# The first half sequence of a state-space recurrence moved into the attention stage before it, with its states summed by adding DMAs, and one expert layer issued at two tiles a unit

## The chip, the cores and the metric

One core of one Trainium2 chip runs the whole program. The engines are PE (matrix multiply; PEld is its weight load), DVE, ACT, POOL (elementwise and activation engines; only PE, DVE and ACT reach PSUM) and SP, which issues most transfers. The metric is device time in microseconds, median of repeated executions: 2376.53 us before (17 runs, 2367.86 to 2383.13).

## The reference, cut to what matters

Four layers over a batch of B = 4 sequences of T = 1024 positions with D = 128 features, in float32; each layer is a mixer and a feed-forward part, each followed by a residual sum and a layer norm. The change touches the third layer and the start of the fourth.

```python
# layer 2 mixer: causal linear attention, 16 heads of 64, q and k weighted by cos and sin of the position
S_cos = S_cos + kc[..., :, None] * v[..., None, :]          # state, step by step over T
num = einsum(qc, S_cos) + einsum(qs, S_sin); den = sum(qc*z_cos + qs*z_sin)
out = num / max(den, 1e-6)
# layer 2 feed-forward: 8 experts, top 2 by softmax; a gated pair and a product per expert
h13 = x @ w13[e]; gate, up = split(h13); y = (silu(gate) * up) @ w2[e]
# layer 3 mixer: a selective state-space recurrence, E = 256 channels, N = 16 states
xs = silu(conv(x @ in_w.T)); delta = softplus(xs @ wd1.T @ wd2.T + b); Bm = xs @ wb.T; Cm = xs @ wc.T
h = exp(delta[:, :, None] * A) * h + (delta * x)[:, :, None] * b[:, None, :]
y = einsum('ben,bn->be', h, c)                              # sum over the 16 states
y = ((y + xs * W_D) * silu(skip)) @ out_w.T
# layer 3 feed-forward: 8 experts, all computed, weighted by a top-p gate
```

## The kernel before

The activations stay in SBUF: `xN[b]` with positions on the partitions, `xT[b]` with features on them.

**Attention (`l2_attn`).** The work is 128 units: for each batch element four quarters of 256 positions, for each quarter eight pairs of heads. The loop runs t from -2 to 131 and issues in each round the parts of neighbouring units: `l2_keys` (t+1: transposes of k into bank `kp`, then kN on ACT), `l2_project` (t+2: q and k in a `pj` bank, r_q and r_k on ACT, the two qt products on POOL, needed two units later), `l2_scores` (t+1: banks pa0 and pa1, then the products `a` on DVE), `l2_before` and `l2_within` (t: all matmuls into the two `po` banks), `l2_sums` (t+1: state sums, bank `kp`, then st on DVE), and `l2_out` (t: dn, its reciprocal and the product co on DVE, which read po). Generators in the list `side` get one step a round: values of the next quarter, `l2_project_out` (transposes and bank `pr`), the norm, and after a batch element's last quarter `l2_dispatch`. PE's order in this loop is the written one (`manual_schedule` for PE); the orders of ACT, DVE, POOL and SP are chosen by a planner from its own simulated times, within the data dependencies.

**PSUM.** There are eight banks of 512 float32 columns. Two are `pj`, two are one tile `po` (of whose banks 130 columns each are used), and four are each shared by two uses: pa0 with m0, pa1 with m1, kp with mo, pr with sx. Accesses of different engines to one bank are put in order, also when they touch different columns.

**Expert layer of layer 2 (`l2_dispatch`, `l2_ffn`).** For each batch element the router ranks the experts (`router`, lines 1220 to 1254), positions are counted, and 16 indirect transfers on POOL scatter the rows to DRAM (L1383). `l2_ffn` is a generator (`moe`) over 4 x 23 = 92 tiles of 128 rows; one step issues the loads for tile t+8, the weights of t+4 (384 KB on SP, L1458, four buffers), the row transposes of t+2, the gated pair of t (`l2_hidden`: m0, m1; tanh on ACT L1490, products on DVE) and the second matmul of t-2 (`l2_expert_out`: mo, ys). After an element's last tile `l2_combine` gathers the rows back with 16 indirect transfers on POOL (L1529) and norms them; then its `st["done"]` is set. In the attention one step a unit is issued, once element 0's rows have been put, until element 1 is done.

**Recurrence (`l3_prepare`, `l3_scan`, `l3_sum`, `l3_finish`).** The 4 x 2 half sequences ("halves") of 512 positions are worked through one after the other, channels on the partitions, two column blocks ec. `l3_prepare` makes xs, delta (`dl`), delta times xs (`ud`), and writes B and C as 32 `rows` to DRAM. `l3_scan` does for each of the 16 states n: two loads on SP that broadcast a row to all partitions (bn, cn, 256 KB each, L1840), db = ud x bn on POOL (L1845), for each ec an exponential on ACT into PSUM (da, L1849) and a scan on DVE (L1850), a copy of the last column to `carry`, hc = db x cn on POOL (L1861). The sum over the states is made on PE by identity matmuls into two banks (pys); for b > 0 two states are first added by an accumulating transfer from POOL's queue (L1865). `l3_finish` applies the gate, the output projection, norm and router, and hands the half to the experts of layer 3 (`l3_experts`, `l3_ffn`: weights wh, matmuls ph and py, ReLU hh), of which each scan step issues three pieces while `moe` has work and four afterwards. Before, half 0 is prepared inside the attention (`l3_early`, at one step a unit once element 0 is done, with its large tiles laid over `xT[0]` to `xT[2]`), and its scan begins after the attention; during it `moe` gets two steps a state, later one.

## Time and profile before

| | us |
|---|---|
| median of 17 runs | 2376.53 (2367.86 to 2383.13) |
| the profiled execution, its own time | 2376.19 |
| its span, first to last instruction | 2374.3 |
| first and last dn of the attention (128) | 646.9 and 1374.1 |
| first db multiply of half 0, half 1, half 2 (POOL) | 1426.3, 1530.9, 1622.5 |
| last hc multiply of half 7 ends | 2233.1 |
| mean granted TensorE clock | 0.909 of full |

In a window's row the columns are: start and end in us from the span's start, its length, then for PE, PEld, DVE, ACT and POOL the busy us and the number of instructions, then the granted TensorE clock, the share of the DMA engines that was busy, and GB/s. In a row of the timeline: start, us, engine, line, operation, tile written <- tiles read, count, and in brackets idle time ahead of it with what ended it. In a row of waits: engine, tile and line that waited, what it waited for, total us, times, longest us. A unit's time is read from one dn to the next (dn is issued once a unit); single units: 36 took 11.2 us (815.2 to 826.4), 68 took 12.1 us, 100 took 13.5 us: in these a router runs. The wait rows of the attention are totals over 640 to 1375 us.

### The profile page before, as it was taken

Reading aid. Unit: us, or ns where it says so; the run is one execution under the profiler, and the core shown is the slowest. Engines: PE = TensorE matmul, PEld = TensorE weight load, DVE = VectorE, ACT = ScalarE, POOL = GpSimd, SP = SyncE. Lnnn points to the kernel's source line nnn. Section 1 sums busy time; section 2 is a strip of 40 time slices with the busy share of each in tenths; the row PEclk is TensorE's granted clock in tenths of the full one; section 3 lists DMA queues with packets and bytes.
Section 4 is the critical chain, followed back from the end, with each engine's and each line's share of the span. In section 5 each row is a group of like instructions: output and inputs, shape, how many; then the busy total and the mean of one; then the engine's idle time right before and its main releaser. Section 6 shows DMA issues by size and latency. Waiting matters only on the chain. (4 is left out here: it accounts for less than half of the span.)

```text
span 2374.3 us, 46470 instructions
## 1 busy us (share of the span) xinstructions
PE 2022.3 (85%) x17858; PEld 1422.1 (60%) x17858; DVE 1349.5 (57%) x3661; ACT 1205.2 (51%) x2619; POOL 1024.3 (43%) x813
## 2 busy tenths in 40 slices
PE   6667979879999999999979857678798989898988
PEld 3455655444477777787767655345565656465666
DVE  7547733433355554655545546785777777577521
ACT  6643424332244443444445535665757776667443
POOL 5001220000123234234143328888897898687500
PEclk9657969979999999999989877899999999899999
DMA  3000110005000010031222046455775667575511
GB/s 103 0 18 19 31 34 1 19 10 167 1 3 3 2 36 22 18 88 40 73 80 76 19 150 186 156 171 166 210 221 141 186 175 191 147 197 160 138 58 49
DMA packets 138702, 211.63 MB, mean 89 GB/s; under 512 B 18613, under 2 KB 75952, under 8 KB 138096
## 3 DMA queue, kind: packets, MB, share of 16 engines
q1 hardware_dynamic: 126192, 173.87, 23.8%
q0 software_dynamic: 12288, 34.79, 6.9%
q8 instruction: 141, 2.31, 0.4%
q14 instruction: 81, 0.66, 0.1%
HBM read 160.29 MB, written 23.16 MB: 77 GB/s over the span
## 5 line engine op out<-in xcount | busy, mean ns | idle before, releaser
L1061 POOL TENSOR_TENSOR qt<-r_q,sb_c_turn 128x256 f32<-128x256 f32 (+1 forms) x256 | 163.9, 661 | 462.1 <-ACT r_q L1053 456.4
L1861 POOL TENSOR_TENSOR hc<-db,cn 128x1024 f32<-128x1024 f32 x128 | 313.5, 2478 | 72.1 <-PE pys L127 31.7
L1845 POOL TENSOR_TENSOR db<-ud,bn 128x1024 f32<-128x1024 f32 x112 | 285.0, 2608 | 32.9 <-DVE ud L1809 16.5
L127 PEld LDWEIGHTS py<-wh,hh 128*128 128x128 f32 x2048 | 251.2, 195 | 72.9 <-issue 37.7
L127 PE MATMUL ph<-xT,wh 128*128 128x512 f32 x512 | 259.0, 622 | 26.9 <-DVE ln_nm L168 6.0
L127 PE MATMUL py<-wh,hh 128*128 128x128 f32 x2048 | 257.1, 279 | 17.9 <-ACT hh L1973 14.6
L1973 ACT ACTIVATE hh<-ph,sb_cols 128x512 f32<-128x512 f32 x256 | 171.5, 681 | 132.7 <-PE ph L127 105.1
L1119 DVE TENSOR_TENSOR a<-pa_m,sb_c_near 128x256 f32<-128x256 f32 x256 | 96.6, 419 | 214.5 <-PE pa_m L127 214.5
L1076 ACT ACTIVATE kN<-kp_mo,sb_c_trig 128x128 f32<-128x128 f32 x448 | 129.7, 371 | 131.8 <-PE kp_mo L131 118.9
L1849 ACT ACTIVATE da<-dl,aneg 128x512 f32<-128x512 f32 x224 | 153.5, 689 | 74.4 <-DVE db L1850 66.9
L127 PE MATMUL pys<-hc,sb_c_ident 128*128 128x512 f32 x320 | 160.7, 627 | 8.9 <-DMA hc<-hc 5.4
L1850 DVE TENSOR_TENSOR_SCAN db<-da,carry,db 128x512 f32<-128x512 f32 x128 | 157.2, 1266 | 11.7 <-ACT da L1849 6.5
L127 PEld LDWEIGHTS ph<-xT,wh 128*128 128x128 f32 x512 | 90.1, 196 | 114.9 <-issue 55.1
L1850 DVE TENSOR_TENSOR_SCAN db<-da,db 128x512 f32<-128x512 f32 x128 | 149.7, 1206 | 8.9 <-ACT da L1849 5.7
L1989 DVE SCALAR_TENSOR_TENSOR h_acc<-py,gt,h_acc 128x128 f32<-128x128 f32 x256 | 71.7, 342 | 135.4 <-PE py L127 135.4
L127 PE MATMUL pqk<-xT,wE 128*128 128x256 f32 x512 | 139.1, 395 | 7.9 <-ACT coT L1195 4.2
L729 POOL DMA_INDIRECT orows<-o,ix x20 | 18.9, 944 | 206.1 <-DVE o L727 175.1
L127 PEld LDWEIGHTS pqk<-xT,wE 128*128 128x128 f32 x512 | 90.3, 197 | 22.5 <-DVE cv L1038 8.1
L127 PEld LDWEIGHTS pys<-hc,sb_c_ident 128*128 128x128 f32 x320 | 60.7, 202 | 70.6 <-issue 57.3
L1195 ACT COPY coT<-pt 128x512 f32<-128x512 f32 x64 | 37.5, 586 | 126.9 <-PE pt L131 126.9
L131 PE MATMUL pt<-sb_c_ident,xN 128*128 128x128 f32 x224 | 54.6, 353 | 52.2 <-ACT xN L174 34.0
L127 PE MATMUL po<-ht,wD 128*128 128x512 f32 x192 | 93.7, 595 | 0.0
(450 smaller groups left out, 4403.1 us busy)
## 6 DMA issues: line engine op xcount, KB each, us to landing
wx<-in_wF SPq DMA_DIRECT2D x92, 384.0 KB
bn<-rows SPq DMA_DIRECT2D x128, 256.0 KB
cn<-rows SPq DMA_DIRECT2D x128, 256.0 KB
wh<-in_wH SPq DMA_DIRECT2D x64, 512.0 KB
hc<-hc POOLq DMA_DIRECT2D x48, 512.0 KB
xrows<-zero SPq DMA_DIRECT2D x4, 1472.0 KB
xg<-xrows SPq DMA_DIRECT2D x20, 256.0 KB
yrows<-ys SPq DMA_DIRECT2D x20, 256.0 KB
```

The costliest lines, as they stand in the source:

```text
L127: return self.nc.tensor.matmul(out=out, lhsT=lhsT, rhs=rhs, start=start, stop=stop)
L131: self.nc.tensor.transpose(out, in_, self.ident[0:n, 0:n])
L1061: nc.gpsimd.tensor_mul(u["qt"][:, m, a:], u["q"][:, a:], c2["turn"][:, m, o + a : o + 2 * P])
L1076: self.nc.scalar.activation(u["kN"][:, c, m, :], pk[:, c, :], AF.Copy, scale=trig[:, k, m : m + 1])
L1119: nc.vector.tensor_mul(u["a"][:, i, :, :], pa[i], self.c2["near"][:, None, :].to_broadcast([P, 2, P]),)
L1195: nc.scalar.copy(oT, pt)
L1845: nc.gpsimd.tensor_mul(db, ud, bc[0])
L1849: nc.scalar.activation(da, dl[:, ec, :], AF.Exp, scale=aneg[:, j : j + 1])
L1850: nc.vector.tensor_tensor_scan(db[:, ec, :], da, db[:, ec, :], carry[:, ec, n : n + 1] if h else 0.0, ALU.mult, ALU.add,)
L1861: nc.gpsimd.tensor_mul(hc, db, bc[1])
L1973: nc.scalar.activation(ht, ph, AF.Relu, bias=self.col("h_b1", i=e * NK + k))
L1989: nc.vector.scalar_tensor_tensor(acc[:, c, :], py[:, c, :], gt[:, c, e : e + 1], acc[:, c, :], ALU.mult, ALU.add,)
```

## The change

Half 0's recurrence is issued inside the attention's loop, followed by half 1's preparation; the layer-3 loop then begins with half 1 and finishes half 0 under it. In detail:

- `l3_early` is a generator now, advanced two steps a round once element 0's experts are done. It prepares half 0 (once element 1 has been routed, since `ud` lies over `xT[1]`), runs `l3_scan_early`, and then prepares half 1 (once element 2 has been routed).
- `l3_scan_early` does the 16 states in five steps each. The exponential and the scan are cut into pieces of 256 columns that use spare columns of the two po banks (da0, da1); the scans of the second piece start from the first one's last column. The sum over states is no longer on PE: y starts as xs x W_D, and each state's product is added to it in SBUF by an accumulating transfer from POOL's queue.
- `early(0)` gives `moe` a second step a round, between `l2_project` and `l2_scores`, while element 0 is not done; `early(1)` is the old step.
- `l2_ffn` is written as queues between its five parts, so that each part follows a fixed number of steps after the one before, and the second matmul one step after the gated pair.
- The router's scratch moves from the bank of pr to spare columns of po and kp; its ranking is done in two halves in the rest of pr's bank instead of a pj bank. `l2_dispatch` loses three of its yields before "put" (one of them in a loop of two, so four steps), and puts two transfers a step.
- co has two buffers instead of three, xnT, tail and xs3 have two in a pool that stays.

Counted in rounds t of the loop, from the generators' yields: element 0's rows are put by round 60 before and 48 after; its first gated pair is at 69 and 53; it is done at 114 and 72; half 0's preparation is at 114 to 125 and 72 to 77; the early scan runs from 77 to 118, half 1's preparation to 123; element 1's combine is issued in the layer-3 loop before and in rounds 115 to 127 after. 45 tiles have their gated pair issued in the loop before, 53 after.

```diff
@@ l2_attn
-            for t, n in dict(pj=2, po=1).items():
+            for t, n in dict(pj=2).items():
...
-            v = two.tile([P, 512], F32, name="pr_sx")
-            self.psq.update(pr=(v, 0), sx=(v, 2 * P))
+            v = two.tile([P, 512], F32, name="pr_q")
+            po = two.tile([P, 2, 512], F32, name="po")
+            self.c2["po"] = po
+            kp = self.psq["kp"][0]
+            self.psq.update(pr=(v, 0), rq=(v, 2 * P), da0=(po[:, 0], 2 * P), da1=(po[:, 1], 2 * P))
+            self.sx = [po[:, 0, 2 * VW :], po[:, 1, 2 * VW :], kp[:, 4 * VW :]]
...
+            def early(b):
+                if all("done" in q for q in self.m2["st"][b:2]) or "put" not in self.m2["st"][0]:
+                    return
+                if b or "done" not in self.m2["st"][0]:
+                    next(moe)
...
+                if t > 0 and "done" not in self.m2["st"][0]:
+                    early(0)
                 if 0 <= t + 1 < n:
                     self.l2_scores(units[t + 1])
...
-                if "put" in self.m2["st"][0] if t > 0 else False:
-                    early(moe)
+                if t > 0:
+                    if "done" not in self.m2["st"][1]:
+                        early(1)
                     if "done" in self.m2["st"][0]:
                         if begin is None:
-                            begin = self.l3_prepare(self.l3_early(first))
-                        next(begin, None)
+                            begin = self.l3_early(first, wp)
+                        for k in range(2):
+                            next(begin, None)
@@ router
+        w = q.shape[1]
+        for c in range(0, n, w):
+            cs = slice(c, c + w)
+            nc.vector.tensor_tensor(q, pj[:, cs], pe[:, cs], ALU.is_equal)
...
@@ l2_ffn
+        steps = (
+            (self.l2_load_rows, 4, True),
+            (self.l2_weights, 2, False),
+            (self.l2_load_tile, 2, True),
+            (self.l2_hidden, 2, False),
+            (self.l2_expert_out, 1, True),
+        )
...
@@ l3
-        halves[0] = dict(self.c3["first"], **{k: halves[0][k] for k in ("prev",)})
-        for i, u in enumerate(halves[1:], 1):
+        halves[0:2] = c3["first"]
+        for i, u in enumerate(halves[2:], 2):
             u["prev"] = halves[i - 1] if u["h"] else None
         work = self.l3_experts(fp)
-        end = iter(())
+        end = self.l3_finish(halves[0])
         for i, u in enumerate(halves):
+            if i == 0:
+                continue
...
-                if i == 0:
+                if i == 1:
                     for k in range(1):
                         next(moe, None)
@@ l3_early
+        for h, u in enumerate(c3["first"]):
+            u["at"], u["prev"] = place(h), c3["first"][0] if h else None
+            while "routed" not in st[1 + h]:
+                yield
+            yield from self.l3_prepare(u)
+            if h == 0:
+                yield from self.l3_scan_early(u, keep, wp, block)
+
+    def l3_scan_early(self, u, keep, wp, block):
+        nc, aneg = self.nc, self.c3["aneg"]
+        dl, ud, rows = u["dl"], u["ud"], u["rows"]
+        u["carry"] = carry = keep.tile([P, 2, NST], F32, name="carry0")
+        u["y"] = y = keep.tile([P, 2, 512], F32, name="y0")
+        for ec in range(2):
+            nc.scalar.activation(y[:, ec, :], u["xs"][:, ec, :], AF.Copy, scale=self.col("W_D", i=ec))
+
+        def fetch(n):
+            ts = []
+            for i in range(2):
+                t = wp.tile([P, 1, 512], F32, name="e_bc", bufs=4)
+                r = i * NST + n
+                nc.sync.dma_start(
+                    out=t[:, 0, :], in_=rows[r : r + 1, :].to_broadcast([P, 512])
+                )
+                ts.append(t.to_broadcast([P, 2, 512]))
+            return ts
+
+        ahead = fetch(0)
+        yield
+        for n in range(NST):
+            bn, cn = ahead
+            db = block()
+            nc.gpsimd.tensor_mul(db, ud, bn)
+            if n + 1 < NST:
+                ahead = fetch(n + 1)
+            yield
+            for ec in range(2):
+                j = ec * NST + n
+                for k in range(2):
+                    ks = slice(k * 256, k * 256 + 256)
+                    da = self.psb(f"da{k}", [P, 256], "da")
+                    nc.scalar.activation(da, dl[:, ec, ks], AF.Exp, scale=aneg[:, j : j + 1])
+                    nc.vector.tensor_tensor_scan(
+                        db[:, ec, ks],
+                        da,
+                        db[:, ec, ks],
+                        db[:, ec, 255:256] if k else 0.0,
+                        ALU.mult,
+                        ALU.add,
+                    )
+                yield
+            nc.scalar.copy(carry[:, :, n : n + 1], db[:, :, 511:512])
+            nc.gpsimd.tensor_mul(db, db, cn)
+            yield
+            nc.gpsimd.dma_start(out=y, in_=db, accum_op=ALU.add)
+            yield
@@ l3_finish
-        yt = u["xs"]
+        yt = u.get("y", u["xs"])
```

## The prediction

> **What bounds the kernel now.** I read the page's slices first, then the stages window by window, then the waits of the stage that receives work. The slices (59.4 us each) show three parts: the front up to about 640 us, the attention from 640 to 1375 us, the last layer from 1426 us on.
>
> ```profile
> PE   6667979879999999999979857678798989898988
> POOL 5001220000123234234143328888897898687500
> PEclk9657969979999999999989877899999999899999
> ```
>
> In the attention PE is at nine tenths and POOL at a quarter; at 1426 us POOL jumps to eight or nine tenths and PE falls. The windows below (PE, PEld, DVE, ACT, POOL busy, granted clock, DMA share, GB/s) are: units 37 to 66 of the attention (no expert tiles), units 69 to 82 (one tile a unit), units 101 to 113 (tiles and batch 0's combine), units 116 to 123 (half 0's preparation), the stretch between the last unit and the first recurrence multiply, then half 0 and half 1 of the recurrence, each from its first db multiply to the next half's.
>
> ```profile
> 826.40:972.30 145.90, 138.92 (x2648) 111.72 (x2643) 78.72 (x276) 62.10 (x182) 58.25 (x89) 0.99 0.08 24
> 989.30:1079.30 90.00, 87.02 (x1466) 73.72 (x1462) 55.43 (x205) 44.43 (x136) 27.85 (x41) 1.00 0.27 77
> 1184.00:1295.60 111.60, 93.09 (x1388) 76.74 (x1384) 56.03 (x219) 58.12 (x172) 40.85 (x54) 0.91 0.26 74
> 1307.70:1355.80 48.10, 40.43 (x710) 31.96 (x706) 26.52 (x78) 21.72 (x51) 19.74 (x25) 0.90 0.07 20
> 1374.50:1426.30 51.80, 27.44 (x167) 25.55 (x165) 19.18 (x79) 17.13 (x46) 14.39 (x15) 0.69 0.51 168
> 1426.30:1530.90 104.60, 75.67 (x289) 47.96 (x288) 69.67 (x114) 65.64 (x148) 91.06 (x51) 0.83 0.57 175
> 1530.90:1622.50 91.60, 65.33 (x275) 40.93 (x275) 67.92 (x124) 53.56 (x107) 77.21 (x40) 0.89 0.53 165
> ```
>
> Per unit that is 145.9/30 = 4.86 us plain, 90.0/14 = 6.43 with a tile, 111.6/13 = 8.58 with the combine, 48.1/8 = 6.01 with the preparation: the attention is PE's own order, and what is added to it costs PE time or a wait. Half 0 is 104.6 us in which POOL is busy 87%: that is what the change takes out of the last layer. The price of one PE wait is seen next: PE's rows around one unit.
>
> ```profile
> 825.78 0.52 PE L1128 MATMUL po<-cv,a 128*64 128x65 f32 x12
> 826.13 0.64 PE L127 MATMUL kp_mo<-cv,kN 128*64 128x65 f32 x16
> 826.70 1.16 PE L1198 MATMUL pr_sx<-wE,coT 128*128 128x128 f32 x8
> 827.86 0.41 PE L131 MATMUL kp_mo<-sb_c_ident,r_k 128*128 128x128 f32 x2
> 828.10 1.03 PE L127 MATMUL pqk<-xT,wE 128*128 128x256 f32 x4
> 829.06 0.67 PE L127 MATMUL pa_m<-r_q,r_k 64*64 64x128 f32 x16
> 829.55 0.41 PE L1128 MATMUL po<-st,qt 64*64 64x65 f32 x16
> ```
>
> PE leaves the po banks at 826.30 and comes back at 829.55: 3.25 us in which others may use them.
>
> **The change, part by part.**
>
> *Out of the last layer: half 0.* Its 32 POOL multiplies (16 x 2.39 + 16 x 2.35 = 75.8 us), 32 scans, 32 exponentials, 32 transfers on SP and 32 identity matmuls (160.7/160 = 1.0 us each) go, and half 1 becomes the first. The stage's whole 104.6 us goes. Counting steps, 53 tiles instead of 45 are issued in the attention's loop, so 39 remain instead of 47; half 1, which had 16, gets 24. Eight more at 6.43 - 4.86 = 1.57 us are 12.6 us of PE in a stage where PE is idle for 26 of 91.6 us; POOL there is at 84%. Bounds 0 and 12.6; I take 6. Sum: -98.6 us.
>
> *The stretch of 51.8 us.* Seven of the tiles were issued by the last loop rounds, four of them after the last unit, some 2.5 us apart; they move into units. POOL's 16 scatters (16 x 1.27 us) still stand ahead of the first multiply. Bounds 0 and -10; taken -6.
>
> *Into the attention, PE's work.* Twelve tiles more within the units: 12 x 1.57 = 19 us (22 if the plain unit is taken at its quietest). Half 1's preparation: units 116 to 123 cost 8 x (6.01 - 4.86) = 9 us over plain, the two after them (15.3 us) 5.6: 15 us, bounds 8 (its matmuls alone, without waits) and 30. Both preparations now go at two steps a unit, where PE's next matmul is half a unit behind the ACT and DVE work it needs: 0 to 10, taken 3.
>
> *Batch 1's combine* ran under half 0 and now falls at units 115 to 127. Batch 0's cost 13 x (8.58 - 6.43) = 28 us, part of it ACT waiting for gathered rows ahead of work for PE. Fewer tiles wait behind it now: bounds 5 and 28, taken 20.
>
> *Two tiles a unit for batch 0*, 12 units: the extra gated pair stands just ahead of the scores, which write the banks that its tanh and products read; in the tile at 1210.35 the last product ends 1.1 us after PE's last gated matmul. 12 x 1.1 = 13 us, bounds 0 and 20. SP's weight loads (384 KB) are asked for two units ahead; PE waited 0.4 us for one in the tail of before.
>
> *Dispatch in fewer steps.* Some 28 DVE operations of about 0.2 us (6 us) fall in one unit, on the po and kp banks, which PE needs every unit; before they stood over five units in a bank that PE writes in half of the units. Three dispatches x 2 us = 6, bounds 0 and 15. The ranking in two halves is the same DVE time; the old one already held PE 3.0 us. The output tile's third buffer: each is read within two units of its filling and needed again after eight, so 0; without that cover, a 0.6 us copy a time.
>
> *The recurrence itself*, 41 units, 2.5 per state. Per state: SP two loads of 256 KB (0.33 us to issue, asked for one state ahead, behind weight loads that may stand for a buffer); POOL two multiplies (4.7 us) and an adding transfer (1.03 us to issue); ACT four 128x256 exponentials (r_q, a 128x256 eviction, takes 0.49) and a carry copy; DVE four 256-long scans (bounds 0.60, half of the 1.21 us row, and 1.21; taken 0.63). Per unit that is POOL +2.3, ACT +0.8, DVE +1.0 us: all three stay under 6 us, so it is waits alone that cost. The exponentials and scans use the po banks, so they wait for PE's last po matmul of the unit and hold its next. Behind a waiting exponential on ACT stand kN and r_q, r_k, behind a scan on DVE the products a and the sums st; PE needs these a unit later. After PE leaves: 0.2 + 0.49 + 2 x 0.63 + the division's 0.16 + 0.18 + 0.42 + gaps 0.3 = 3.0 us with one column block in the unit, inside the 3.25; with both (one unit of five, 8 in all) about 4.45, so 1.2 us over: 10 us. POOL's qt products (0.7 us each) stand behind multiplies of 2.4 us but are needed two units later. With scatters and gathers on POOL in the same units I add 5. Total 15; the lower bound is 0 and the upper 60 (1.5 us in every one of 41 units, the chain doubled by late neighbours). The adding transfers each wait for the one before, 12 us earlier; the chain of waits has such a transfer at 4.55 and 6.17 us, so nothing.
>
> Sum: -98.6 - 6 + 19 + 15 + 3 + 20 + 13 + 6 + 15 = -13.6 us. The profiled execution took 2376.19 us (span 2374.3), within 0.4 us of the median of 17 runs (2376.53): **2363 us**.
>
> Two rules of the Trainium skill, for the reader; no number above needs them. PE waits that fit the first, on other columns of a bank, stand in the trace:
>
> ```profile
> PE kp_mo L131 <- DVE st L1103: 14.6, 14, 2.7
> PE kp_mo L127 <- DVE st L1103: 13.7, 7, 3.4
> PE pr_sx L1198 <- DVE rt_g L1250: 9.1, 3, 3.0
> ```
>
> "PSUM — Partial Sum Buffer", section "PSUM bank collisions raise a hardware error", says to guard by bank and quadrant, not by address, reads among them: it speaks against lending po's spare columns to the recurrence. Were addresses enough, the recurrence would cost 5 instead of 15 and the sum be 2353. "DMA: Bandwidth & Descriptors", section "Anatomy of one DMA — SWDGE (gpsimd) path", fits 2.0 us + bytes/436 GB/s, an estimate of 3.2 us for 512 KB where the chain shows 4.55; by either the transfer is done before the next, and the sum stays.
>
> **The rivals.**
>
> *Well hidden.* All terms at their gaining ends: -104.6 - 10 + 19 + 8 + 0 + 5 + 0 + 0 + 0 = -82.6, 2294 us. For it: DVE and ACT are at about half in the units. Against it: batch 0's combine shows what queued work costs PE.
>
> *The po banks become the bound (slower).* One mechanism: exponentials and scans that hold the po banks past PE's return. At its upper bound of 60 us the sum is 2363 + 45 = 2408. It decides from 15 + 13.6 = 28.6 us on, that is 0.70 us in each of the 41 units. For it: ACT and DVE queues are in order, and one late kN or scan delays all. Against it: four units of five hold one column block or none, and leave 0.25 us or more to spare.
>
> *The last layer gives it back.* If from half 1 on PE sets the pace (it is busy 85 to 92% in halves 2 to 7), only its removed work comes off: 32 x 1.0 identity matmuls + 8 of preparation + 8 x 1.57 = 52.6 instead of 98.6: 2409 us. Against it: PE is idle 29 us in half 0, and the order from half 1 on is the same as before.
>
> That the recurrence doesn't fit at all is excluded by the count: two steps a unit from unit 72 end it at unit 118, and half 1's preparation at 123, of 127.
>
> **How the numbers follow.** About 0.2% (4.8 us) is what a measurement of this kernel can tell from no change. Forecast 0.42 (own range 2345 to 2385: 0.29 faster, 0.08 same, 0.05 slower); well hidden 0.24, all faster; po banks 0.20, slower; given back 0.14 (0.11 slower, 0.02 same, 0.01 faster). Together faster 0.54, same 0.10, slower 0.36. From 2316 (the well hidden case's upper half kept) to 2408 about 2 in 10 is left out.
>
> **What would show it.** The last dn of the attention some 85 us later than 1374.1; first db multiply of half 1 about 46 us after it; from there to the end some 850 us (843.4 before). Units 77 to 118 near 5.2 us without a tile; PE waits on po from scans of about 10 us in all; scans of 256 at 0.63. The forecast is wrong if po waits pass 29 us, if the combine stalls PE far from 20, or if half 1 takes more than 105 us.

## The result, and the profile after

The changed kernel takes 2457.6 us (median of 8 runs, 2453.95 to 2460.66) against 2376.69 before (median of 46, 2365.7 to 2383.86): a ratio of 1.0341, with a 95% interval of 1.0325 to 1.0357. It is 81 us slower; the forecast had 14 us faster. The profiled execution took 2452.53 us (span 2450.7).

The page's slices (now 61.3 us each):

```profile
PE   6677889979899888767877768576989889798988
POOL 5002210000232241235553742589768989597500
PEclk9667989979999899978899988687999999899999
```

The attention, 640 to 1535 us, has lost its nines on PE: from the fourteenth slice on it reads 6 to 8, while POOL has risen to 5 and 7 in places. The last layer looks as before.

Two windows of each kernel settle where the time went: first dn to last dn, and last dn to the end. Before:

```profile
646.90:1374.10 727.20, 665.62 (x11636) 544.75 (x11631) 394.07 (x1362) 337.86 (x970) 234.53 (x355) 0.96 0.13 38
1374.10:2374.30 1000.20, 837.55 (x4087) 559.53 (x4087) 634.06 (x1286) 615.20 (x1152) 698.60 (x368) 0.92 0.56 160
```

After:

```profile
640.00:1535.50 895.50, 730.55 (x11813) 588.36 (x11809) 467.43 (x1536) 416.94 (x1157) 339.18 (x419) 0.93 0.22 58
1535.50:2450.70 915.20, 771.50 (x3847) 519.25 (x3846) 570.74 (x1179) 558.57 (x1015) 608.73 (x320) 0.92 0.56 157
```

The attention grew by 168.3 us and what follows it shrank by 85.0. Take PE's busy time (the first number after the length) from the length: PE's busy time went up by 64.9 us in the first window and down by 66.1 in the second. That the two nearly cancel doesn't mean that work only moved. About half of the 66.1 are half 0's identity matmuls, which the change does away with; the whole program's rows for them, before and after, are 35.7 us apart:

```profile
L127 PE MATMUL pys<-hc,sb_c_ident 128*128 128x512 f32 x320 | 160.7, 627 | 8.9 <-DMA hc<-hc 5.4
```

```profile
L127 PE MATMUL pys<-hc,sb_c_ident 128*128 128x512 f32 x256 | 125.0, 615 | 3.2 <-DMA hc<-hc 2.5
```

So about 30 us of work moved into the attention, and by the difference about 35 of its 64.9 came without more work: the attention's own matmuls take longer there (the 512 of pqk 411 ns in the mean, 395 before), at a mean granted clock of 0.93 instead of 0.96. PE's idle time went up from 61.6 to 165.0 us in the attention (+103) and down from 162.7 to 143.7 after it (-19). The loss is in the attention, most of it PE idle time; of the last layer's idle time only 19 us went.

Stage by stage, after (plain units 0 to 36; units 52 to 65 with two tiles; 77 to 101 and 101 to 118 with the states; 118 to 127; the stretch after the last unit; half 1; half 2):

```profile
640.00:808.30 168.30, 160.84 (x3082) 127.69 (x3079) 89.52 (x294) 73.82 (x221) 47.77 (x85) 1.00 0.01 3
906.60:1023.80 117.20, 98.28 (x1405) 82.77 (x1403) 52.40 (x187) 45.66 (x142) 16.76 (x31) 0.99 0.29 84
1133.20:1320.80 187.60, 144.60 (x2256) 118.26 (x2254) 107.46 (x314) 93.61 (x248) 93.38 (x94) 0.89 0.35 89
1320.80:1465.70 144.90, 107.49 (x1699) 88.19 (x1699) 73.09 (x240) 68.28 (x201) 82.51 (x81) 0.92 0.39 98
1465.70:1535.50 69.80, 56.39 (x819) 44.26 (x814) 39.94 (x129) 45.26 (x99) 18.03 (x23) 0.88 0.15 41
1535.50:1547.70 12.20, 7.70 (x51) 6.59 (x50) 4.55 (x21) 6.80 (x22) 0.02 (x1) 0.90 0.30 86
1547.70:1659.10 111.40, 77.54 (x338) 55.77 (x339) 84.84 (x169) 58.82 (x116) 90.31 (x49) 0.75 0.61 190
1659.10:1794.00 134.90, 106.17 (x551) 72.93 (x550) 81.74 (x157) 83.61 (x176) 96.67 (x57) 0.91 0.67 187
```

The same units took 168.3, 59.1, 144.8, 134.7 and 55.4 us before. The first 36 units did not change by a tenth of a us. Half 1 and half 2 took 91.6 and 101.1.

PE's waits in the attention of the changed kernel, the rows that answer the three shown before (14.6, 13.7 and 9.1 us there):

```profile
PE kp_mo L127 <- DVE st L1109: 32.4, 23, 3.9
PE pr_q L1203 <- DVE rt_r L1262: 22.1, 3, 9.1
PE kp_mo L131 <- DVE st L1109: 20.8, 18, 4.2
PE pt L131 <- DVE co L1178: 13.1, 8, 2.8
PE kp_mo L127 <- DVE st L1106: 11.1, 15, 1.9
PE po L1134 <- DVE co L1178: 10.2, 4, 3.6
PE pa_m L127 <- DVE mh L1507: 8.5, 12, 2.8
```

The largest are not on po, which the forecast watched. They are on kp: PE wants to write that bank while DVE still has to read the state sums st from it. PE's rows in two-tile units of the changed kernel show how it comes about:

```profile
924.92 0.64 PE L127 MATMUL kp_mo<-cv,kN 128*64 128x65 f32 x16
926.55 0.71 PE L127 MATMUL kp_mo<-wx,mh 128*128 128x128 f32 x4 [1.00 <-DVE st L1109]
927.10 1.06 PE L127 MATMUL pa_m<-xgT,wx 128*128 128x128 f32 x8
...
934.60 0.71 PE L127 MATMUL kp_mo<-wx,mh 128*128 128x128 f32 x4 [0.90 <-DVE st L1106]
935.15 1.06 PE L127 MATMUL pa_m<-xgT,wx 128*128 128x128 f32 x8
```

The state sums go into kp, and the very next instruction is a tile's second matmul into the same bank; only then comes the gated pair (pa_m), 1.06 us of work that needs another bank. The rewritten expert loop runs its five parts last first.

### The profile page after: what moved, and what is told of

Same layout as the page of the kernel before. It is cut to its first block, busy times and chain, and to the rows that moved or that the text cites. A ratio compares the mean times of both kernels' runs of the same rounds, so it can differ in the third digit from the quotient of the medians.

```text
span 2450.7 us, 46174 instructions
## 1 busy us (share of the span) xinstructions
PE 2017.5 (82%) x17794; PEld 1420.3 (58%) x17794; DVE 1360.4 (56%) x3727; ACT 1227.4 (50%) x2668; POOL 1039.1 (42%) x829
## 4 chain that ended last, share of the span: by engine, by line
PE 36%; DVE 17%; ACT 10%; issue 5%; DMA 3%; POOL 3%; another core or an unknown queue 1%; ACTq 0%; DVEq 0%; SPq 0%; POOLq 0%
PE py L127 6%; DVE db L1938 5%; PE ph L127 5%; PE po L1134 5%; PE pa_m L127 4%; PE pqk L127 4%; PE kp_mo L127 2%; PE pys L127 2%; PE pr_q L1203 2%; PE pv L127 2%; ACT da L1937 1%; DMA y<-e_db 1%; PE pt L131 1%; PE kp_mo L131 1%
## 5 line engine op out<-in xcount | busy, mean ns | idle before, releaser
L1949 POOL TENSOR_TENSOR hc<-db,cn 128x1024 f32<-128x1024 f32 x112 | 274.5, 2493 | 65.2 <-PE pys L127 34.4
L1933 POOL TENSOR_TENSOR db<-ud,bn 128x1024 f32<-128x1024 f32 x96 | 246.5, 2618 | 63.2 <-ACT dl L1898 34.1
L1937 ACT ACTIVATE da<-dl,aneg 128x512 f32<-128x512 f32 x192 | 131.5, 689 | 71.9 <-DVE db L1938 71.1
L127 PE MATMUL pqk<-xT,wE 128*128 128x256 f32 x512 | 145.8, 411 | 8.0 <-ACT coT L1200 3.6
L127 PE MATMUL pys<-hc,sb_c_ident 128*128 128x512 f32 x256 | 125.0, 615 | 3.2 <-DMA hc<-hc 2.5
L1938 DVE TENSOR_TENSOR_SCAN db<-da,db 128x512 f32<-128x512 f32 x96 | 112.1, 1205 | 5.0 <-ACT da L1937 2.6
L127 PE MATMUL pa_m<-r_q,r_k 64*64 64x128 f32 x2048 | 96.5, 295 | 9.7 <-DVE mh L1507 8.5
L1134 PE MATMUL po<-cv,a 128*64 128x65 f32 x2048 | 93.0, 233 | 3.4 <-issue 3.3
L1134 PE MATMUL po<-st,qt 64*64 64x65 f32 x3584 | 84.2, 227 | 13.7 <-DVE co L1178 10.2
```

The costliest lines, as they stand in the source:

```text
L127: return self.nc.tensor.matmul(out=out, lhsT=lhsT, rhs=rhs, start=start, stop=stop)
L1134: self.nc.tensor.matmul(out=u["po"][self.HALF[j], i, c, :], lhsT=lhsT, rhs=rhs, start=key not in u["begun"], stop=True, skip_group_check=True,
L1933: nc.gpsimd.tensor_mul(db, ud, bc[0])
L1937: nc.scalar.activation(da, dl[:, ec, :], AF.Exp, scale=aneg[:, j : j + 1])
L1938: nc.vector.tensor_tensor_scan(db[:, ec, :], da, db[:, ec, :], carry[:, ec, n : n + 1] if h else 0.0, ALU.mult, ALU.add,)
L1949: nc.gpsimd.tensor_mul(hc, db, bc[1])
```

## The experiments

Chips differ (the kernel before took 2343.5 us on one, 2384.1 on another), so results are given as ratios to the kernel before on the same chip, and 0.01 of a ratio is 23.8 us. After "+-" stands the half width of a 95% interval, for a difference of two ratios combined from both as a root of squares.

### What half 0's states cost in the last layer

`f1_before_no0`: the kernel before, without the work of half 0's states.

```diff
+        if b == h == 0:
+            nc.gpsimd.memset(carry, 0.0)
+            for n in range(NST):
+                yield
+            return
         for n in range(NST):
             bc = []
```

> The kernel before, without half 0's sixteen states in the last layer (y is xs x W_D alone, the handed-on state zero); its sixteen rounds of other work (two tiles, half 1's preparation) stay where they were. The forecast let the whole stage of 104.6 us go and added 6 for the tiles, which supposes that POOL sets the stage's time: what is left on PE there is 75.7 - 32 x 1.0 = 44 us, so 61 us less, ratio 0.974. Theory 'PE's work is conserved and only its idle time can be won': 32 us of identity matmuls and about 15 to 20 of the 29 idle, 47 to 52 us, ratio 0.979. Theory of the rival 'given back': only the 32 us of matmuls, 0.987.

Measured 0.9822 (0.9797 to 0.9846): 42 us, between the theory of 47 to 52 us and that of 32. The stretch and half 0 together, before and without the states:

```profile
1374.10:1530.90 156.80, 103.51 (x457) 73.91 (x457) 89.18 (x195) 82.77 (x194) 105.45 (x65) 0.78 0.55 173
```

```profile
1376.80:1501.10 124.30, 75.93 (x381) 62.83 (x381) 54.01 (x162) 58.77 (x141) 30.88 (x34) 0.71 0.49 145
```

POOL lost 75 us of work and the window only 32.5. PE lost 27.6, and its idle time went from 53.3 to 48.4. POOL was the busiest engine there, and the stage did not get shorter by what was taken off it: work of others (tiles, gathers, a preparation) runs through the same time with its own chains.

### One part of the change after another

Five kernels without half 0's states take the rest of the change off piece by piece.

`e1_noscan`: the changed kernel, with the body of `l3_scan_early` behind the two lines that set y replaced.

```diff
+        nc.gpsimd.memset(carry, 0.0)
+        yield
-        ahead = fetch(0)
...
-            nc.gpsimd.dma_start(out=y, in_=db, accum_op=ALU.add)
```

> Left out: half 0's sixteen states; y is only xs x W_D and the state handed to half 1 is zero. Everything else of the change stays (both preparations, two tiles a unit, the routers, the dispatch). Against the changed kernel's 2457.6 us: the forecast's price for the recurrence in the attention (15, at most 60) gives 2443, at the least 2398. Theory 'the scan makes DVE and ACT late for PE's other banks': units 77 to 118 were 53 us longer than before, so about 2405. Theory 'tiles and routers, not the scan': 2450 or more. Units 77 to 89, 7.45 us each now, should come to about 5.9 by the second theory and stay above 7 by the third.

`e2_noscan_one`: and one tile a unit.

```diff
-                if t > 0 and "done" not in self.m2["st"][0]:
-                    early(0)
```

> As e1_noscan (half 0's sixteen states left out), and in addition one tile a unit for batch element 0. Against e1_noscan: the forecast's price of the second tile is 13 us, so 13 faster. Theory 'the second tile stalls PE': units 52 to 65 were 58 us longer than before, of which 12 x 1.57 = 19 is the tiles' own work, so about 39 faster. Theory 'the tiles' work is only moved': within 5 us. Units 52 to 65 should come to about 59 us by the first two if one tile a unit is what they held before.

`h3_base`: and routers and dispatch as before.

```diff
-            self.sx = [po[:, 0, 2 * VW :], po[:, 1, 2 * VW :], kp[:, 4 * VW :]]
+            self.sx = [v[:, 2 * P :], v[:, 2 * P + 96 :], v[:, 2 * P + 160 :]]
...
-            q = self.psb("rq", [P, n // 2, NE * NE], "prq")
+            q = ps([P, n, NE * NE], "prq")
```

and in `l2_dispatch` the yields that the change took out ahead of the puts:

```diff
         nc.vector.tensor_sub(base, end.rearrange("p e o -> p o e"), nt.rearrange("p e o -> p o e"))
+        yield
...
         nc.vector.tensor_copy(st["eti"], et)
+        yield
...
             st["wts"].append(v)
+            yield
```

> Half 0's states left out, one tile a unit for element 0, the router's scratch and the dispatch's yields as before: what stays of the change is the new order inside the expert layer's loop, half 1's preparation inside the attention, and half 1 as the first half of the last layer. If the prices add up: 1.0136 (e2_noscan_one) - 0.0134 (1.0341 - 1.0207, routers and dispatch) = 1.0002. The kernel before without the same states is at 0.9822, so 43 us would be left for these three. By the forecast's terms (15 + 3 + 20 + 19 - 6 + 6 against the preparation, combine and tiles leaving the last layer) it should be no slower than 0.982.

`i4_base_fwd`: and the order within a step of the expert loop.

```diff
-            for i, (step, gap, near) in reversed(list(enumerate(steps))):
+            for i, (step, gap, near) in enumerate(steps):
```

> As h3_base (half 0's states left out, one tile a unit, routers and dispatch as before; 1.0031), with the order within a step of the expert layer's loop as before and the loop otherwise new. h4_base_ffn, with the whole old loop, stood at 0.9799. Theory 'order alone': 0.980 to 0.985, and PE's waits for st ahead of the second matmul go from 63.6 us in 41 to about 12. In the whole changed kernel the order was worth 1.1% (wide interval); if the second matmul meets st only in the step after the state sums, which every tile takes here and half of element 0's there, it should be worth 30 to 45 us here. Theory 'the waits for rows': 0.995 or above.

`h4_base_ffn`: and the whole expert loop as in the kernel before.

```diff
-        steps = (
...
+        for t in range(-8, n + 4):
+            while t + 8 < n and "put" not in units[max(t + 8, 0)]["st"]:
...
+            if 0 <= t < n:
+                self.l2_hidden(units[t], wp)
+            if 0 <= t - 2 < n:
...
```

> As h3_base (half 0's states left out), with the expert layer's loop in its old order too. Theory 'the new order is dear' (its gated pair and second matmul stand one step apart instead of two, its parts are run last first): 20 us or more below h3_base. Theory 'it is where the combines and the preparation fall': within 5 us of it. No term of the forecast speaks of the order.

| kernel | ratio to before | step to the row above, in us of 2376.7 |
|---|---|---|
| before, no states (`f1_before_no0`) | 0.9822 (0.9797 to 0.9846) | -42 +- 6 from before itself |
| `h4_base_ffn` | 0.9799 (0.9764 to 0.9834) | -5 +- 10: half 1 prepared in the attention, half 1 first, eight tiles more in the attention, smaller buffers |
| `i4_base_fwd` | 0.9875 (0.9852 to 0.9898) | +18 +- 10: an element doesn't wait for the next one's rows |
| `h3_base` | 1.0031 (1.0013 to 1.0049) | +37 +- 7: the reversed order |
| `e2_noscan_one` | 1.0136 (1.0094 to 1.0178) | +25 +- 11: routers and dispatch |
| `e1_noscan` | 1.0159 (1.0118 to 1.0200) | +5 +- 14: the second tile a unit |
| the changed kernel | 1.0341 (1.0325 to 1.0357) | +43 +- 10: the states in the attention |

The first row against the last but one is the finding: with the same states left out of both, the changed kernel is 80 us slower than the one before. That is the whole of the loss, and it comes from what the change does beside the recurrence.

The states cost 42 +- 6 us in the last layer and 43 +- 10 in the attention, so moving them gained nothing that these runs can tell. The largest single step beside that is one word, `reversed`. PE's waits for st ahead of the second matmul in the units with tiles, in `h3_base`, `i4_base_fwd` and `h4_base_ffn`:

```profile
PE kp_mo L127 <- DVE st L1107: 63.6, 41, 5.6
```

```profile
PE kp_mo L127 <- DVE st L1107: 27.9, 16, 3.7
```

```profile
PE kp_mo L127 <- DVE st L1107: 12.5, 6, 3.3
```

PE's rows at that place of a unit, in `h3_base` and then in `h4_base_ffn`:

```profile
993.88 0.64 PE L127 MATMUL kp_mo<-cv,kN 128*64 128x65 f32 x16
995.51 0.71 PE L127 MATMUL kp_mo<-wx,mh 128*128 128x128 f32 x4 [0.99 <-DVE st L1107]
996.06 1.06 PE L127 MATMUL pa_m<-xgT,wx 128*128 128x128 f32 x8
```

```profile
990.57 0.64 PE L127 MATMUL kp_mo<-cv,kN 128*64 128x65 f32 x16
991.13 1.16 PE L127 MATMUL pa_m<-xgT,wx 128*128 128x128 f32 x8
992.20 0.71 PE L127 MATMUL kp_mo<-wx,mh 128*128 128x128 f32 x4
```

In the old order the gated pair covers DVE's reading of the bank, and the second matmul starts with no wait; in the new one PE stands 1.0 us. The remaining 18 us of the loop are not settled: `i4_base_fwd` has 32 gathers of combines inside the attention and `h4_base_ffn` 16, so this step also moves element 1's combine in, which the forecast priced at 20; no run separates the two.

### The order, undone in the whole change

`i1_fwd` is the changed kernel with `reversed` taken out, `i2_fwd_rd` has routers and dispatch as before too, `h5_cand` has these and the whole old loop, `i3_fwd_rd_one` is `i2_fwd_rd` with one tile a unit. The edits are those shown above; `i1_fwd` is this line alone:

```diff
-            for i, (step, gap, near) in reversed(list(enumerate(steps))):
+            for i, (step, gap, near) in enumerate(steps):
```

> The changed kernel whole, with one word of the expert layer's loop undone: within a step its five parts are issued in the order rows, weights, transposes, gated pair, second matmul, as before, and no longer the reverse; the distances in steps stay. Theory 'the reversed order': the second matmul writes the bank kp straight after the state sums, whose copies st DVE has yet to read; in h3_base PE waited 63.6 us in 41 waits for st there, in h4_base_ffn 12.5. Undone, some 30 to 50 us come off: ratio 1.013 to 1.021 from 1.0341. Theory 'what costs in the new loop is that element 0 no longer waits for element 1's rows, so that combines and preparations fall elsewhere': 1.030 or above.

> As i1_fwd, with the router's scratch and the dispatch's yields as before too; the states in the attention and the two tiles a unit stay. If the prices add up: i1_fwd's ratio less 0.0134, that is 1.000 to 1.008. The forecast's sum without its dispatch term would be 2357, 0.992. If the waits overlap (the router's and the second matmul's are for the same engine, DVE), less comes off: up to 1.015.

> As e10_router_disp (1.0207), with the whole loop of the expert layer as before: the old order within a step, and element 0's last tiles wait until element 1's rows are put. Theory 'order alone': the same as i2_fwd_rd within 5 us. Theory 'the waiting for rows matters': it differs by more than 10 us either way, since element 0 is done later and the states end later in the attention, or after it.

> The whole recurrence as in i2_fwd_rd (order, routers and dispatch as before; 1.0156), but one tile a unit for element 0. Leaving out the second tile was worth 0.2% without the states. Theory 'the second tile costs 13 us and nothing depends on it': 1.010. Theory 'it is what lets the states end inside the attention': element 0 is done some 12 units later, the last states fall behind the last unit with no attention work beside them, and at 2 steps a unit some 10 units' worth is left: 20 to 40 us more, 1.024 to 1.032.

`i1_fwd` came to 1.0231 (1.0156 to 1.0306), 26 +- 18 us less than the changed kernel; its attention was 21 us shorter, and the wait shown first above went from 32.4 to 14.0 us:

```profile
PE kp_mo L127 <- DVE st L1109: 14.0, 11, 4.1
```

`i2_fwd_rd` came to 1.0156 (1.0108 to 1.0204), the best whole version, 44 +- 12 us less. Order (26) and routers with dispatch (32, below) would make 58 if they added up; the intervals leave it open whether they do. `h5_cand` came to 1.0365 (1.0317 to 1.0413) and `i3_fwd_rd_one` to 1.0264 (1.0243 to 1.0286), although their attentions are shorter (816 and 784 us against 837): element 0 is done later in both, the last states fall behind the last unit, and from there to the first multiply of half 1 it is 98 and 104 us instead of 29. The second tile a unit and the loop that doesn't wait are what make the states fit inside the attention.

### Routers and dispatch

`e3_router` is the changed kernel with only the router's scratch and ranking as before; `e10_router_disp` has the dispatch's yields too (the two edits shown for `h3_base`).

> The changed kernel whole, with the router's scratch back in the bank of pr and the ranking back in a pj bank in one piece. The forecast held that the new places cost nothing in the router and 6 us in the dispatch: 2452 to 2458. Theory 'ranking in pr's bank holds PE': the units with routers (36, 68, 100) were 4.3, 9.0 and 8.1 us longer, in sum 21, so about 2437; PE's wait for pr on the ranking (22 us in 3 waits) should go back to about 9.

> The changed kernel whole with the router's scratch and ranking as before (as in e3_router) and the dispatch's four yields back. e3_router alone shortened the attention by 13.7 us. The forecast has the compressed dispatch at 6 us (0 to 15): a ratio to before of about 1.0275 from e3_router's 1.0300. Theory 'the dispatch's DVE work costs the same in one unit or in five': 1.0300. A dispatch that ends four rounds later also puts element 1's rows later, which could give 2 to 5 us back to the units after it.

`e3_router`: 1.0300 (1.0256 to 1.0344), 10 +- 11 us; its attention is 13.7 us shorter. `e10_router_disp`: 1.0207 (1.0185 to 1.0230), 32 +- 7 us. The ranking in pr's bank held PE 22.1 us in three waits; back in a pj bank, in `e3_router`:

```profile
PE pr_q L1203 <- DVE rt_g L1260: 10.9, 3, 4.9
```

So spreading the dispatch over four more rounds is worth about 22 +- 12 of the 32. Part of that may be that element 0's tiles then begin later (16 instead of 23 of them in units 52 to 65); the run doesn't separate it.

### What the states' price in the attention is made of

`e4_da_sbuf`: exponentials to SBUF, not to po's spare columns.

```diff
-                    da = self.psb(f"da{k}", [P, 256], "da")
+                    da = wp.tile([P, 256], F32, name="e_da", bufs=2)
```

> The changed kernel whole, with the 64 exponentials of half 0 written to SBUF (two buffers of 256 columns) instead of the spare columns of the po banks. Theory of the forecast (po banks cost 10 of the 15): about 2448. Theory 'the lent banks are the whole of the scan's price': 2457.6 - 50 = about 2408. Theory 'it is DVE's and ACT's own queues, whatever the bank': 2453 or more, and PE's wait for the state sums st (kp bank) stays at some 60 us.

Measured 1.0400 (1.0361 to 1.0440), 14 +- 10 us slower than the changed kernel. With no bank to wait for, the planner runs all sixteen states in 157 us instead of 307 (first scan to last; the groups of the scan in the changed kernel and in `e4_da_sbuf`):

```profile
L1787 DVE TENSOR_TENSOR_SCAN e_db<-po,e_db x64: 679/714/751, 1148.5 to 1455.6; 128x256 f32<-128x256 f32 x64
```

```profile
L1787 DVE TENSOR_TENSOR_SCAN e_db<-e_da,e_db x64: 654/750/2844, 1151.4 to 1308.6; 128x256 f32<-128x256 f32 x64
```

The units beside them become slower (units 77 to 101 take 222.8 us instead of 187.6), and units 101 to 118 faster (123.7 instead of 144.9). Taking the lent banks away did not take the price away; the banks had paced the states. What the banks alone would cost at the same pace, the run doesn't show. The section "PSUM bank collisions raise a hardware error" of the Trainium skill's "PSUM — Partial Sum Buffer" asks that engines be kept apart bank by bank; this kernel does so, and here freedom from the bank was worth nothing.

`e6_nodve` leaves out exponentials and scans alone:

```diff
-                    da = self.psb(f"da{k}", [P, 256], "da")
-                    nc.scalar.activation(da, dl[:, ec, ks], AF.Exp, scale=aneg[:, j : j + 1])
-                    nc.vector.tensor_tensor_scan(
...
```

`h1_pool` the carry copies too:

```diff
-            nc.scalar.copy(carry[:, :, n : n + 1], db[:, :, 511:512])
```

`h2_nopool` keeps these and leaves out POOL's part:

```diff
-            nc.gpsimd.tensor_mul(db, ud, bn)
...
-                        db[:, ec, ks],
+                        ud[:, ec, ks],
...
-            nc.gpsimd.tensor_mul(db, db, cn)
-            nc.gpsimd.dma_start(out=y, in_=db, accum_op=ALU.add)
```

> Left out of the changed kernel: the 64 exponentials and 64 scans of half 0, so that its states are products without a recurrence. POOL's 32 multiplies, the loads on SP, the adding transfers and the carry copies stay. Leaving the states out whole gave 1.0159 of before, the changed kernel 1.0341: the states cost some 43 us. Theory 'DVE and ACT are made late by exponentials and scans' (also the forecast's po-bank account): the ratio comes to about 1.018, units 77 to 89 to about 5.9 us. Theory 'POOL, busy half of the time with multiplies and transfers, makes qt and the scatters late': it stays at 1.030 or above, units 77 to 89 above 7.

> As e6_nodve (half 0's exponentials and scans left out), and the carry copies left out too: in e6_nodve they stood on ACT's queue for 61 us behind POOL's multiplies and put a wait of their own there. POOL's 32 multiplies, the loads and the adding transfers stay. The states whole cost 43 us (1.0341 against 1.0159). Theory 'POOL's work and its transfers are the price': 1.030 or above again. Theory 'e6_nodve measured only its own new wait, the price is DVE's and ACT's work': about 1.018.

> The counterpart: half 0's 64 exponentials, 64 scans (which read delta times xs in place of the multiplied block) and carry copies stay; POOL's 32 multiplies, the 32 loads and the 16 adding transfers are left out, so y stays xs x W_D. Theory 'the lent banks and the scans' queues are the price' (the forecast's account, whose 15 us are all of this part): 1.030 or above. Theory 'POOL's work is the price': about 1.018. If the two parts add up, this and h1_pool stand together 1.8% above 1.0159.

`e6_nodve` gave 1.0331 (1.0299 to 1.0362), as if DVE's and ACT's part cost nothing. That reading was wrong: the run had made a wait of its own, the carry copy on ACT behind POOL's multiply, with kN and r_q behind it.

```profile
ACT carry L1787 <- POOL e_db L1777: 61.0, 15, 9.7
```

Without that copy `h1_pool` gave 1.0260 (1.0223 to 1.0297), and `h2_nopool` 1.0255 (1.0220 to 1.0291). Over 1.0159 that is 24 +- 13 us for POOL's part and 23 +- 13 for DVE's and ACT's, 47 together where the whole is 43. The second is borne out by the trace: in `h2_nopool` PE waited 13.2 us on po and 11.8 on pt for co on DVE, against none on po and 3.9 us on pt without the states. The first isn't, since `h1_pool` too has a wait of its own. Half 1's preparation begins on ACT with a write into a block that the last adding transfer still holds, and behind ACT's 17 us a reciprocal and the state sums on DVE were late for PE:

```profile
1276.30 0.31 ACT L1802 ACTIVATE e_db<-xN 128x128 f32<-128x128 f32 x1 [17.00 <-DMA y<-e_db]
1280.29 1.22 PE L127 MATMUL kp_mo<-wx,mh 128*128 128x128 f32 x4 [20.39 <-DVE st L1109]
```

In the changed kernel ACT waited 4.8 us at that place. That POOL's part is half of the price is therefore an estimate by subtraction (43 less 23, 20 +- 17), not shown by a run. POOL's waits in the changed kernel, units 77 to 118, show one thing that the forecast excluded:

```profile
POOL e_db L1777 <- DMA y<-e_db: 43.3, 12, 5.8
POOL e_db L1797 <- ACT carry L1796: 30.1, 11, 5.2
```

and PE's in `h1_pool`, where only POOL's part is left, show one way in which PE pays:

```profile
PE po L1134 <- POOL qt L1067: 16.2, 10, 4.1
```

The next state's multiply waits for the adding transfer to let go of its block, of which there are two, and qt stands behind the multiply. In the changed kernel itself PE waited for qt only once, 2.5 us, so this chain is a small part of the price there.

What else the price is made of, the attentions of the changed kernel and of `e1_noscan` show side by side (one execution each, 895.5 and 854.5 us). The waits on kp are the same without the states, and so is the one on the ranking (22.1 us in both); `e1_noscan` has

```profile
PE kp_mo L127 <- DVE st L1109: 32.4, 23, 3.5
PE kp_mo L131 <- DVE st L1109: 21.1, 18, 5.1
PE pt L131 <- DVE co L1178: 3.9, 3, 2.8
```

With the states PE waits 19.4 us more for co (po 10.2 instead of nothing, pt 13.1 instead of 3.9), and its busy time is 730.6 instead of 715.9 us for the same 11813 matmuls. These two are 34 of the 41 us.

### Two that were to gain something

`e11_combine` ends the second tile with element 0's last tile, so that its combine goes at half the rate.

```diff
-                if t > 0 and "done" not in self.m2["st"][0]:
+                if t > 0 and "last" not in self.m2["st"][0]:
                     early(0)
```

> The changed kernel whole, but the second step a round ends with element 0's last tile, so that its combine goes at half the rate (the preparation and the states begin some five units later). Theory 'combine 0 crowded into units 65 to 72 holds PE': these units were 27 us longer than before, 9 of it the router; a slower combine gives 5 to 10 us back, ratio about 1.031. Theory 'its price is the same at either rate, as the forecast took it (20 us a combine wherever it stands)': 1.034, the time only moves to units 72 to 80. A later end of the states (unit 123 instead of 118) may cost up to 10 us, ratio 1.038.

1.0392 (1.0364 to 1.0420): 12 +- 8 us slower. The attention is 9.3 us shorter, and the stretch after it 11.6 us longer, half 2 4.7: work pushed past the last unit costs more than it saved.

`g1_quads` is the kernel before with four instead of two states added by transfers in halves 2 to 7.

```diff
-            if n % 2 and b > 0:
+            if n % 4 and b > 0:
```

> The kernel before, with the change's own device used where PE is short: in the last layer's halves 2 to 7 four states instead of two are first added by transfers, so that 8 identity matmuls a half fall away (1.0 us each, 48 us of PE in six halves) and 4 adding transfers a half are added (1.03 us each to issue on POOL, 25 us). Theory 'PE's work sets the last layer's pace': up to 40 us less, ratio 0.983. Theory 'POOL or the chain of transfers takes over' (POOL is busy 82% there, a transfer took 4.6 to 6.2 us, the buffers of hc are four): 1.00 or above.

1.0092 (1.0063 to 1.0121), 22 us slower. PE was busy 25 us less between 1530 and 2150 us, but now waits for the transfers that feed the sums, 15 us more in that window; the rest of the loss is not explained. Before and then `g1_quads`:

```profile
PE pys L127 <- DMA hc<-hc: 5.4, 2, 3.9
```

```profile
PE pys L127 <- DMA hc<-hc: 20.0, 2, 10.3
```

No version that does all the work beat the kernel before; the three below it in time (`f1_before_no0`, `h4_base_ffn`, `i4_base_fwd`) leave out half 0's states.

## Why the prediction was wrong

The forecast's sum was -13.6 us and the measurement is +81. By its own terms:

| term | forecast | measured | from |
|---|---|---|---|
| half 0 out, the stretch, 12 tiles, preparation, denser preparations | -98.6 - 6 + 19 + 15 + 3 = -67.6 | -48 +- 8 | `h4_base_ffn` against before |
| batch 1's combine | +20 | +18 +- 10, with the loop's not waiting | `h4_base_ffn` to `i4_base_fwd` |
| two tiles a unit | +13 | +5 +- 14 | `e2_noscan_one` to `e1_noscan` |
| dispatch 6, ranking 0 | +6 | +25 +- 11 (32 +- 7 with the states) | `h3_base` to `e2_noscan_one`; `e10_router_disp` |
| the recurrence | +15 | +43 +- 10 | `e1_noscan` to the changed kernel |
| the order inside the loop's step | not priced | +37 +- 7 | `i4_base_fwd` to `h3_base` |

The measured column adds up to 80 us. It prices each part in one order of taking them off: in the whole change the reversed order alone came to 26 +- 18 us instead of 37. The first row's `h4_base_ffn` has eight tiles more in the attention than before, not twelve.

**The step that failed first is the twelve tiles, "12 x 1.57".** A tile was priced from units of the kernel before and taken as the same thing after, while the diff shows its five parts reversed. The working followed each bank through the routers and the recurrence, but not through the loop: state sums into kp, second matmul into kp, st on DVE between them. So the order got no term, though it makes every tile in the attention dearer, also the 40 that were there before: 37 us over the 48 tiles of `h3_base`, about 0.8 us a tile. In units 52 to 65, 58.1 us for 23 tiles are 2.53 each, where the forecast's 1.57, and 1.1 more for a second tile, make about 49; `i1_fwd` took 104.0 us there instead of 117.2, so 13 of the 58 are the order. The text ahead of the prediction also has the second matmul one step behind the gated pair; the distance in the diff belongs to the part that precedes, and it is two steps, as before. What changed is the order, and that an element doesn't wait for the next one's rows.

**"The stage's whole 104.6 us goes" was too much.** The states' part of the stage is 42 us (`f1_before_no0`), and the rest of the stage is work that has to be done elsewhere. From the last dn to the end 85.0 us came off, where the stage and the stretch were to give 98.6 + 6 = 104.6; 66.1 of it is PE's busy time (36 of identity matmuls that are gone, the rest work that went into the attention), 19 idle time. The rival "the last layer gives it back" had the mechanism nearer (what PE does is removed, its idle time hardly), with -58.6 for stretch and halves; the truth lies between. Half 1 was to take up the moved work at +6 us: halves 1 and 2 took 53.6 us more together, the stretch 39.6 less. It also fell past the mark of 105 us that the forecast set for half 1 (111.4).

**The recurrence's price was mis-sized, 15 for 43, and its place was in part wrong.** Scans on po: PE waited there 10.2 us for co and a few us for other reasons, about what was written. Two things got no term: co was late for pt as well (9.2 us more than without the states), and PE took about 15 us longer over the same matmuls. The waits on kp and pr are not the recurrence's: without the states they are as long. The rival's threshold of 28.6 us was passed without its mechanism. "The adding transfers ... nothing" failed as a statement on POOL, which waited 43.3 us for them; what of this reached PE in the changed kernel is not shown beyond 2.5 us at qt. The 256-long scan, taken at 0.63, took 0.71.

**The dispatch and the ranking.** "The ranking in two halves is the same DVE time" left out that its bank is now the one PE needs for the output projection: the wait went from 9.1 to 22.1 us. Its 0 and the 6 for the dispatch are 25 to 32.

**What held.** Two tiles a unit: PE waited 8.5 us in 12 waits on the gated pair's banks, where 12 times 1.1 were written, and taking the second tile away was worth no more than that. Batch 1's combine at 20 doesn't contradict the 18, in which the loop's not waiting has an unknown part, and the counts (52 tiles within the units, the states' end at the 118th) came as counted. The last dn came 161 us later where 85 were written, to which the order, the dispatch with the routers, and the recurrence each gave their part.

## What to carry to other kernels

Before pricing a step from the old trace, check in the diff that the step still has the same neighbours: two instructions on one bank whose order is swapped cost here about 0.8 us a tile. Set PE's busy time against the length of each stage, before and after, and count the matmuls too: what this change could win was work that goes for good (36 us of identity matmuls) and idle time that goes (19 us of 163), and it lost more than both where the same matmuls took longer and waited. An engine's busy time (POOL's 87%) is not what a stage costs; leave its work out and measure, since here 75 us less on it made its stretch 32 us shorter.

## What the runs showed of the hardware that was not expected

The granted TensorE clock was lower where PE had gaps: 0.89 in units 77 to 101 with the states (PE busy 77% of the time), 0.95 in the same units of `e1_noscan` without them (83%), 1.00 in the plain units (96%). The states in the attention give PE nothing to do, and still its busy time was 730.6 us with and 715.9 without them, for 11813 matmuls in both: by these two executions some 15 of the 43 us are the same matmuls taking longer. It isn't a rule by busy share alone: units 52 to 65 were granted 0.99 at 84%.

In `h1_pool` the adding transfers into y (512 KB) took 4.6 us from issue to landing in the median, those into hc in the last layer 6.8. By the fit in the section "Anatomy of one DMA — SWDGE (gpsimd) path" of the Trainium skill's "DMA: Bandwidth & Descriptors" (2.0 us and the bytes at 436 GB/s), 512 KB come to an estimate of 3.2 us, which is short of both; the measurement decides.
